# A graph layer on one core: single-column copies of x by 16-bit addresses, VectorE's written as maxima, and more of them

## The chip, the core and the metric

The kernel runs on one core of a Trainium2 chip. The core's engines work side by side: TensorE (PE) multiplies matrices, VectorE (DVE) works on elements and reductions, ScalarE (ACT) on activation functions and copies, GpSimd (POOL) issues the gathers, and SyncE (SP) only issues DMAs. Each has its own queue of instructions and works it off in order. The metric is the device time in microseconds (us) of one execution; smaller is better.

## The reference

A layer of a graph network over 12,500 nodes with 64 features and 400,000 edges with 16 attributes each. The edges come sorted by their target `dst`; the sources `src` are in random order.

```python
m_in = concatenate([x[src], x[dst], edge_attr], -1)       # 64 + 64 + 16
h = silu(m_in @ W1 + b1)                                  # 400000 x 64
messages = silu(h @ W2 + b2)
agg = segment_sum(messages, dst, num_segments=12500)
gnn = silu(concatenate([x, agg], -1) @ W3 + b3)
out = layernorm(x + gnn)
```

Everything is float32. The costly part is `x[src]`: 400,000 rows of 256 bytes at random places.

## The kernel before, in words

**Tiles.** The edges are cut into 3,125 tiles of 128. Eight tiles make an oct (1,024 edges), the unit of the main loop (391 octs, `for o in range(NO + 1)`). Three octs (24 tiles) make a window; since the edges are sorted by target, the targets of a window lie within 112 neighbouring nodes. Work on an oct is spread over several turns of the loop: its data are loaded two turns ahead (`load(o + 2)`), its messages are computed in turns o and o + 1, and summed in turn o + 2.

**Per oct.** SyncE loads `dr`, the target indices repeated over 112 partitions (L370, 448 KB), and the attributes into the lower part of `oh` (L372, 64 KB). VectorE makes the one-hot matrix `oh` of targets against the window's nodes (L381) and `eh`, its counterpart with edges on partitions (L388). TensorE multiplies `oh` with the window's `xw`, which holds x of the window's nodes by its part of W1 and the attributes' part below it (L401), and adds the sources' part (L412, L415). ScalarE makes `h` (L419), TensorE the second layer (L428, L430), ScalarE `m` (L434), and TensorE adds the messages by `eh` into a window's sums in PSUM (L443). At a window's end VectorE adds the sums into `agg` (L448), which holds all nodes. A window's own nodes are loaded by `window_load` (L347 register, L351 DMA), multiplied by `window_product` (L356) and put in place by `window_copy` (L360, L362). As soon as a group of nodes has all its sums, its last layer and layer norm are done between the octs (`node_load` to `store`, entered by `later`).

**Three ways to the sources' rows.** At the start TensorE multiplies all of x with the sources' part of W1 into a table `pa` in DRAM (`table`); the first 9 octs (`RAW`) gather from x itself.

1. *Gathers* (`gather`, L341): GpSimd fetches the 128 rows of a tile from `pa` with one indirect DMA into `ga`, three octs ahead, into five buffers. TensorE brings them into place by multiplying with the identity (L415).
2. *Columns* (`columns`, L267): x transposed stands in SBUF as `xs`, one column of 64 values for each node. An edge's column is copied from there by ScalarE or VectorE into `cx`, one instruction for each edge: 64 partitions by 4 bytes, with the source address in a register. 256 edges make a pair of tiles, which TensorE then multiplies with W1 (L412), and for which no gather is made. In each oct ScalarE copies 28 + 28 columns (`ACOLS`: one part before `h`, one before `m`), VectorE 24 + 24 (`VCOLS`). The addresses come as indices by a SyncE load (L319), are turned into addresses by VectorE (L327, two instructions for each pair, as the two halves of a pair read from two copies of x), and are loaded into the engines' registers by a TensorLoad (L263), at most 16 (`ALOAD`) at a time on ScalarE. 104 columns an oct make a pair for every 2.46 octs, 153 pairs in all.
3. *Rows* (`rows`, L292): SyncE fetches 16 rows of `pa` in each oct with 16 DMAs of one row, again by addresses in registers (L288). 23 pairs come this way.

**x in SBUF.** `xs` holds x transposed twice, on partitions 0 to 63 for even tiles and on 64 to 127 for odd ones. The address in a register has the partition in its upper bits (`XBASE`) and the byte in the partition, from 35,840 on (`XADDR`), in its lower ones; it is an int32. Seven loads for each copy (`resident`) are issued on SyncE's queue in the first octs.

**Order.** The order of instructions on PE, ACT, DVE and SP is that of the program text (`manual_schedule`); waits follow from the data and from the pools' buffers (`bufs`). GpSimd only gathers, and runs ahead as far as the five `ga` buffers let it. At the end the kernel makes sure that every edge was within its window; if not, a second general program does the work, which does not happen with this input.

## Time and profile before

| | us |
|---|---|
| median of 7 runs | 4874.31 (4853.41 to 4893.45) |
| profiled execution | 4867.82 |
| its span | 4866.0 |
| ScalarE busy | 2752.3 |
| VectorE busy | 2621.9 |
| GpSimd busy | 2648.1 |
| TensorE busy | 2936.0 |

The span is the time between the first and the last instruction in the profile. A row of the groups reads: line, engine, operation, what it writes and reads, how many, then busy time and the mean in ns of one, then the idle time of the engine just before these instructions and what ended most of it ("issue" is an idle time that ended by nothing that the profile shows; "remote" is a release by a semaphore whose sender isn't found). Register loads, semaphores and the issuing of DMAs aren't counted as busy. In the views of waits a row is the engine and line that waited, what for, then microseconds in all, times, and the longest. In the views of stretches each row is a stretch from and to, its length, then for PE, PEld (weight loads), DVE, ACT and POOL the busy time and the number of instructions, TensorE's granted clock, the share of the DMA engines and GB/s. In a timeline a row is the start, the length, engine, line, operation and count, and in brackets the idle time before.

### The profile page before, as it was taken

How to read it: one execution, taken by the hardware profiler on the slowest of the kernel's cores; microseconds unless marked ns; L12 is line 12 of the kernel's file. 1: busy time of each engine (PE TensorE's matmuls, PEld its weight loads, DVE VectorE, ACT ScalarE, POOL GpSimd, SP SyncE). 2: the span in 40 equal slices, each digit the busy share in tenths (PEclk: the TensorE clock that was granted, in tenths of full speed). 3: DMA queues.
4: the chain of work that ended last, by engine and by line, in shares of the span. 5: the costliest groups of instructions: out<-in, count | busy, mean ns of one | idle time of the engine just before them, and what ended most of it. 6: DMA issues, size and time to landing. Idle time of an engine off the chain costs nothing. (4 is left out here: it accounts for less than half of the span.)

```text
span 4866.0 us, 96997 instructions
## 1 busy us (share of the span) xinstructions
PE 2936.0 (60%) x15387; PEld 1956.7 (40%) x15387; DVE 2621.9 (54%) x19955; ACT 2752.3 (57%) x21941; POOL 2648.1 (54%) x2782
## 2 busy tenths in 40 slices
PE   4556656656666655665655556656655566566666
PEld 3334434434444443443433334434434344344444
DVE  1355555555555555555555555555555555555555
ACT  1255656656555555555555565555555556556554
POOL 5455555555555555555555555555555555555553
PEclk6766766666666666666666666676666666666667
DMA  4322222222222222222222222222222222222222
GB/s 104 95 65 66 62 65 66 67 65 66 65 69 69 66 65 65 66 62 67 68 60 70 64 67 66 66 66 66 62 64 71 66 66 65 64 62 66 68 72 55
DMA packets 199259, 327.19 MB, mean 67 GB/s; under 512 B 94959, under 2 KB 103306, under 8 KB 197722
## 3 DMA queue, kind: packets, MB, share of 16 engines
q1 hardware_dynamic: 96142, 226.51, 14.9%
q0 software_dynamic: 88736, 91.04, 10.7%
q10 hardware_dynamic: 13740, 3.32, 0.3%
q14 instruction: 511, 4.19, 0.3%
q8 instruction: 130, 2.13, 0.2%
HBM read 314.20 MB, written 6.40 MB: 66 GB/s over the span
## 5 line engine op out<-in xcount | busy, mean ns | idle before, releaser
L341 POOL DMA_INDIRECT ga<-pa,sc x2701 | 2578.8, 955 | 2112.5 <-PE p L415 1047.4
L267 ACT COPY cx<-xs 64x4 uint8 x21112 | 2270.1, 188 | 1421.3 <-issue 1363.7
L267 DVE COPY cx<-xs 64x4 uint8 x18056 | 1516.7, 192 | 781.6 <-issue 690.7
L443 PE MATMUL pg<-eh,m 128*64 128x112 f32 x6250 | 608.7, 365 | 1693.8 <-ACT m L434 812.2
L443 PEld LDWEIGHTS pg<-eh,m 128*64 128x64 f32 x6250 | 486.8, 201 | 1778.6 <-ACT m L434 851.4
L381 DVE TENSOR_TENSOR oh<-dr,wrow 112x1024 f32<-112x1024 int32 x391 | 476.0, 1217 | 907.9 <-DMA dr<-in_dst_row 567.5
L430 PE MATMUL p<-w2d,h 128*128 128x128 f32 x3126 | 719.2, 402 | 0.0
L430 PEld LDWEIGHTS p<-w2d,h 128*128 128x128 f32 x3126 | 617.0, 294 | 147.7 <-issue 147.7
L401 PE MATMUL p<-oh,xw 128*64 128x512 f32 x1564 | 645.7, 918 | 4.8 <-issue 4.8
L415 PEld LDWEIGHTS p<-ident,ga 128*128 128x128 f32 x2702 | 444.2, 247 | 304.6 <-issue 263.8
L415 PE MATMUL p<-ident,ga 128*128 128x128 f32 x2702 | 506.2, 341 | 0.0
L388 DVE TENSOR_TENSOR eh<-wrow,dc 128x896 f32<-128x896 f32 x391 | 424.4, 1085 | 140.6 <-issue 85.1
L419 ACT ACTIVATE h<-p,b1s 128x512 f32<-128x512 f32 x391 | 267.5, 684 | 297.7 <-remote 157.4
L434 ACT ACTIVATE m<-p 128x512 f32<-128x512 f32 x391 | 231.7, 593 | 344.0 <-remote 191.8
L428 PE MATMUL p<-b2r,one 3*128 3x512 bf16 x391 | 211.5, 541 | 0.0
L356 PE MATMUL mm<-w1ab,xr 64*112 64x64 f32 x262 | 76.3, 388 | 129.8 <-DMA xr<-in_xt 83.1
L412 PEld LDWEIGHTS p<-cx,w1d 128*128 128x128 f32 x306 | 59.8, 245 | 199.8 <-issue 199.8
L401 PEld LDWEIGHTS p<-oh,xw 128*64 128x64 f32 x1564 | 103.1, 182 | 67.2 <-issue 38.9
L356 PEld LDWEIGHTS mm<-w1ab,xr 64*112 64x112 f32 x262 | 53.2, 257 | 161.1 <-DMA xr<-in_xt 108.5
L341 POOL DMA_INDIRECT ga<-in_x,sc x72 | 68.1, 946 | 51.6 <-PE mm L406 29.3
L412 PE MATMUL p<-cx,w1d 128*128 128x128 f32 x306 | 95.4, 403 | 0.0
L448 DVE TENSOR_TENSOR agg<-agg,pg 128x112 f32 x131 | 34.8, 266 | 94.2 <-issue 39.0
(73 smaller groups left out, 734.2 us busy)
## 6 DMA issues: line engine op xcount, KB each, us to landing
dr<-in_dst_row SPq DMA_DIRECT2D x390, 448.0 KB
rx<-pa SPq DMA_DIRECT2D x5888, 0.2 KB
ga<-pa,sc POOLq DMA_INDIRECT x2701
oh<-in_attr_t SPq DMA_DIRECT2D x390, 64.0 KB
xs<-in_xt SPq DMA_DIRECT2D x12, 512.0 KB
xr<-in_xt SPq DMA_DIRECT2D x131, 28.0 KB
pa<-v ACTq DMA_DIRECT2D x24, 128.0 KB
xa<-in_x SPq DMA_DIRECT2D x24, 128.0 KB
```

The lines of the kernel that those rows point to most:

```text
L267: copy(t[h, 4 * e:4 * e + 4], xb[h, ds(r - (XBASE[s] + XADDR), 4)])
L341: nc.gpsimd.indirect_dma_start(out=ga[:, i, :], out_offset=None, in_=x if o < RAW else pa[:, :], in_offset=bass.IndirectOffsetOnAxis(ap=sc ...
L381: nc.vector.tensor_tensor(oh[0:W, :n2 * P], dr[:, :n2 * P], wn[0:W, c:c + 1].to_broadcast([W, n2 * P]), op=OP.is_equal)
L388: nc.vector.tensor_tensor(eh[:, :n], winrow[c][:, None, :].to_broadcast([P, n, W]), dc[:, t0:t0 + n, None].to_broadcast([P, n, W]), op=OP. ...
L401: nc.tensor.matmul(p1[s * D:(s + 1) * D, :k], xw[c % 3], ohv[:, s, :k], start=True, stop=False, skip_group_check=True)
L412: nc.tensor.matmul(p1[:, 0, :], w1d, cols.pop(o), start=False, stop=False, skip_group_check=True)
L415: nc.tensor.matmul(p1[:, i, :], g2.rearrange("p s d -> p (s d)"), ident, start=False, stop=(i == k - 1), skip_group_check=True)
L419: nc.scalar.activation(h[:, :k], p1[:, :k], AF.Silu, bias=b1s)
L428: nc.tensor.matmul(p2[:, :n2, :], one3, b2r[:, :n2, :], start=True, stop=False, skip_group_check=True)
L430: nc.tensor.matmul(p2[:, 2 * i:2 * i + 2, :].rearrange("p s d -> p (s d)"), h[:, i, :], w2d, start=False, stop=(i == k - 1), skip_group_ch ...
L434: nc.scalar.activation(m[:, :n2], p2[:, :n2], AF.Silu)
L443: nc.tensor.matmul(pg[s * D:(s + 1) * D, :], m[:, i, :], eh[:, i, :], start=(first and i < 2), stop=(last and i >= n - 2), skip_group_chec ...
```

## The change

All of it concerns the second way, the columns, and what stands around it:

- x transposed stands once in SBUF, on partitions 0 to 63, and at the front of it (pool `front`, from byte 8,864 of a partition on). Both halves of a pair read from it. The addresses fit in 16 bits; VectorE writes them with one instruction for each pair into a 16-bit tile `cxa` (L333), and the register loads read 16-bit words.
- VectorE's column copies become `tensor_reduce` with a maximum over one byte (L273); ScalarE's stay copies (L275).
- ScalarE copies 32 + 32 columns in an oct, VectorE 32 + 24. 120 columns make a pair for every 2.13 octs, 177 pairs instead of 153. So there are 24,192 copies instead of 21,112 on ScalarE, 21,120 instead of 18,056 on VectorE, and 48 gathers less.
- The loads of x into SBUF, now seven instead of 14, and the second load of `dc` go from SyncE's to ScalarE's queue.
- `ehp` has five buffers instead of four, `win` three instead of two, `cxi` two instead of three. A window's load stands one oct earlier; its product stands at the head of the turn before its first oct, ahead of the columns, instead of at the end of the turn before that; the window's sums are added one oct later, and the node work follows by one oct more.
- The scratch tiles of the check at the end lie in `agg` instead of `xs`. The ring in SBUF for the descriptors of GpSimd's DMAs is 8,192 bytes instead of 16,384, which lets x begin so far in front.

```diff
-ACOLS = (28, 28)
-VCOLS = (24, 24)
+ACOLS = (32, 32)
+VCOLS = (32, 24)
-XBASE = (0, 64 << 18)
-XADDR = 35840
+XADDR = 8864
...
+    front = ctx.enter_context(tc.tile_pool(name="front", bufs=1))
+    xs = front.tile([D, NP], F32, name="xs")
...
-    def resident(s, c):
+    def resident(c):
         w = min(XC, NP - c)
-        nc.sync.dma_start(xs[s * D:(s + 1) * D, c:c + w], xt[:, c:c + w])
+        nc.scalar.dma_start(xs[:, c:c + w], xt[:, c:c + w])
...
-            tc.tile_pool(name="ehp", bufs=4) as ehp, \
-            tc.tile_pool(name="work", bufs=2) as work, tc.tile_pool(name="win", bufs=2) as win, \
+            tc.tile_pool(name="ehp", bufs=5) as ehp, \
+            tc.tile_pool(name="work", bufs=2) as work, tc.tile_pool(name="win", bufs=3) as win, \
...
                 _, regs = nc.values_load_multi_w_load_instructions(
-                    indices[j][0:1, e0:e0 + n], engines=(eng,), min_val=XBASE[s] + XADDR,
+                    addresses[j][0:1, e0:e0 + n], engines=(eng,), min_val=XADDR,
...
                 for e, r in zip(range(e0 % P, e0 % P + n), regs):
-                    copy(t[h, 4 * e:4 * e + 4], xb[h, ds(r - (XBASE[s] + XADDR), 4)])
+                    to, frm = t[h, 4 * e:4 * e + 4], xb[:, ds(r - XADDR, 4)]
+                    if eng == ENG.DVE:
+                        nc.vector.tensor_reduce(to, frm[:, :, None], AX.X, OP.max)
+                    else:
+                        nc.scalar.copy(to, frm)
...
-                t = indices[j]
-                for s in range(2):
-                    h = slice(s * P, (s + 1) * P)
-                    nc.vector.tensor_scalar(t[:, h], t[:, h], 4.0, float(XBASE[s] + XADDR), op0=OP.mult, op1=OP.add)
+                addresses[j] = cxa.tile([1, 2 * P], U16, name="cxa")
+                nc.vector.tensor_scalar(addresses[j], indices.pop(j), 4.0, float(XADDR), op0=OP.mult, op1=OP.add)
...
                 if o == 8:
-                    nc.sync.dma_start(dc[:, SCT:], dst_c[:, SCT:])
+                    nc.scalar.dma_start(dc[:, SCT:], dst_c[:, SCT:])
...
-                    if octs[o + 2][3]:
-                        window_load(octs[o + 2][0])
+                if o + 3 < NO and octs[o + 3][3]:
+                    window_load(octs[o + 3][0])
+                if o and o + 1 < NO and octs[o + 1][3]:
+                    window_product(octs[o + 1][0])
                 if o + 1 < NO:
                     compare_dst(o + 1)
                 columns(o, ENG.DVE, 0)
-                if o >= 3 and octs[o - 3][4]:
-                    add_window(octs[o - 3][0])
+                if o >= 4 and octs[o - 4][4]:
+                    add_window(octs[o - 4][0])
...
-                if o + 2 < NO and octs[o + 2][3]:
-                    window_product(octs[o + 2][0])
...
-    nc = bacc.Bacc("TRN2", target_bir_lowering=False, num_devices=1)
+    nc = bacc.Bacc("TRN2", target_bir_lowering=False, num_devices=1, dynamic_dma_scratch_size=8192)
```

More of the change, by code (lines that the diff above doesn't have):

```diff
@@ L13 @@
 U8 = mybir.dt.uint8
+U16 = mybir.dt.uint16
 AF = mybir.ActivationFunctionType
@@ L102, in windows @@
     assert W + A == P and N + W <= NP
+    front = ctx.enter_context(tc.tile_pool(name="front", bufs=1))
+    xs = front.tile([D, NP], F32, name="xs")
+    assert XADDR + 4 * N < 1 << 16
     const = ctx.enter_context(tc.tile_pool(name="fconst", bufs=1))
@@ L164, in windows @@
     XC = 2048
-    xs = fast.tile([P, NP], F32, name="xs")
-    def resident(s, c):
+    def resident(c):
         w = min(XC, NP - c)
-        nc.sync.dma_start(xs[s * D:(s + 1) * D, c:c + w], xt[:, c:c + w])
+        nc.scalar.dma_start(xs[:, c:c + w], xt[:, c:c + w])
     def table(c):
@@ L176, in table @@
             o = c + i * P
-            nc.tensor.matmul(ps[:, i, :], xs[0:D, o:o + P], w1ab[:, 0, :], start=True, stop=True)
+            nc.tensor.matmul(ps[:, i, :], xs[:, o:o + P], w1ab[:, 0, :], start=True, stop=True)
         t = v[:, c // (4 * P) % (2 * RB)]
@@ L227, in windows @@
             tc.tile_pool(name="psa", bufs=1, space=PSUM) as psa, \
-            tc.tile_pool(name="cx", bufs=4) as cx, tc.tile_pool(name="cxi", bufs=3) as cxi, \
+            tc.tile_pool(name="cx", bufs=4) as cx, tc.tile_pool(name="cxi", bufs=2) as cxi, tc.tile_pool(name="cxa", bufs=4) as cxa, \
             tc.tile_pool(name="rx", bufs=2) as rx, tc.tile_pool(name="rxi", bufs=2) as rxi, \
@@ L240, in windows @@
             pairs.append(o)
-        cols, indices = {}, {}
+        cols, indices, addresses = {}, {}, {}
         xb = xs.bitcast(U8)
@@ L248, in columns @@
             if eng == ENG.Activation:
-                lo, n, copy = lo + sum(ACOLS[:part]), ACOLS[part], nc.scalar.copy
+                lo, n = lo + sum(ACOLS[:part]), ACOLS[part]
             else:
-                lo, n, copy = lo + sum(ACOLS) + sum(VCOLS[:part]), VCOLS[part], nc.vector.tensor_copy
+                lo, n = lo + sum(ACOLS) + sum(VCOLS[:part]), VCOLS[part]
             hi = lo + n
@@ L263, in columns @@
                 _, regs = nc.values_load_multi_w_load_instructions(
-                    indices[j][0:1, e0:e0 + n], engines=(eng,), min_val=XBASE[s] + XADDR,
-                    max_val=XBASE[s] + XADDR + 4 * (N - 1), skip_runtime_bounds_check_because="src names a node")
+                    addresses[j][0:1, e0:e0 + n], engines=(eng,), min_val=XADDR,
+                    max_val=XADDR + 4 * (N - 1), skip_runtime_bounds_check_because="src names a node")
                 for e, r in zip(range(e0 % P, e0 % P + n), regs):
-                    copy(t[h, 4 * e:4 * e + 4], xb[h, ds(r - (XBASE[s] + XADDR), 4)])
+                    to, frm = t[h, 4 * e:4 * e + 4], xb[:, ds(r - XADDR, 4)]
[3 more added lines that the diff above has]
+                        nc.scalar.copy(to, frm)
                 lo += n
@@ L472, in node_product @@
             av = agg[:, c:c + n].rearrange("k (p i) -> k i p", i=G)
-            xv = xs[0:D, c:c + n].rearrange("k (p i) -> k i p", i=G)
+            xv = xs[:, c:c + n].rearrange("k (p i) -> k i p", i=G)
             nc.tensor.matmul(po[:p], ones[:, :p], b3r, start=True, stop=False, skip_group_check=True)
@@ L527, in windows @@
         for q in range(early):
-            o = lead[due[q]] + 2
+            o = lead[due[q]] + 3
             later(o, node_load, q)
@@ L531, in windows @@
             later(o, node_silu, q)
-            later(o + 1, node_stats, q)
+            later(o + 2, node_stats, q)
         for q0 in range(0, rest, RB):
-            o = lead[due[q0 + RB - 1]] + 2
-            later(o + 2, root, q0, q0 + RB)
-            later(o + 3, inverse, q0, q0 + RB)
+            o = lead[due[q0 + RB - 1]] + 3
+            later(o + 3, root, q0, q0 + RB)
+            later(o + 4, inverse, q0, q0 + RB)
             for r in range(RB):
-                later(o + 3 + 2 * r, divide, q0 + r)
-                later(o + 4 + 2 * r, store, q0 + r)
+                later(o + 4 + 2 * r, divide, q0 + r)
+                later(o + 5 + 2 * r, store, q0 + r)
         for o in range(min(AHEAD, NO)):
@@ L563, in windows @@
                     for c in parts[:3] if o == 0 else parts[o + 2:o + 3]:
-                        resident(0, c)
+                        resident(c)
                 if o == 8:
-                    nc.sync.dma_start(dc[:, SCT:], dst_c[:, SCT:])
+                    nc.scalar.dma_start(dc[:, SCT:], dst_c[:, SCT:])
                 if o == RAW:
@@ L569, in windows @@
                     nc.vector.memset(eps, 1e-5)
-                if 5 <= o < 5 + (len(parts) + 1) // 2:
-                    for c in parts[(o - 5) * 2:(o - 4) * 2]:
-                        resident(1, c)
                 index(o + 3)
@@ L609, in windows @@
                         f(*a)
-        off = xs[:, :TILES]
+        off = agg[:, :TILES]
         full = (TILES // CT) * CT
@@ L620, in windows @@
         nc.gpsimd.iota(evi, pattern=[[STEP, NCH]], base=0, channel_multiplier=0)
-        lag = xs[:, TILES:TILES + NCH]
+        lag = agg[:, TILES:TILES + NCH]
         nc.vector.tensor_tensor(lag, evi, wb, op=OP.subtract)
@@ L637, in windows @@
         add_up(NO - 1)
-        for o in range(NO - 2, NO):
+        for o in range(NO - 3, NO):
             if octs[o][4]:
```

## The prediction

> **What bounds the kernel now.** I read the page's totals first, then the costliest groups, then what each engine waits for between 300 and 4,700 us (start and end left out), then single stretches in the order of time. The totals and the groups:

> ```profile
> PE 2936.0 (60%) x15387; PEld 1956.7 (40%) x15387; DVE 2621.9 (54%) x19955; ACT 2752.3 (57%) x21941; POOL 2648.1 (54%) x2782
> L341 POOL DMA_INDIRECT ga<-pa,sc x2701 | 2578.8, 955 | 2112.5 <-PE p L415 1047.4
> L267 ACT COPY cx<-xs 64x4 uint8 x21112 | 2270.1, 188 | 1421.3 <-issue 1363.7
> L267 DVE COPY cx<-xs 64x4 uint8 x18056 | 1516.7, 192 | 781.6 <-issue 690.7
> L381 DVE TENSOR_TENSOR oh<-dr,wrow 112x1024 f32<-112x1024 int32 x391 | 476.0, 1217 | 907.9 <-DMA dr<-in_dst_row 567.5
> ```

> No engine is busy over 60%, so the bound is in how the instructions follow each other. 4,866 us over 391 octs is 12.44 us for an oct. The waits, engine by engine:

> ```profile
> ACT cx L267 <- issue: 1295.1, 1894, 5.5
> ACT m L434 <- remote: 169.4, 46, 7.7
> ACT h L419 <- remote: 119.0, 34, 5.5
> ```

> ```profile
> POOL ga L341 <- PE p L415: 1012.4, 223, 14.5
> POOL ga L341 <- issue: 641.0, 2098, 0.6
> ```

> ```profile
> SPq L292 <- DMA rx<-pa: 54.8, 113, 1.4
> SPq L319 <- ACTq L263: 3.1, 11, 0.7
> ```

> GpSimd waits 1,012 us for a gather buffer that TensorE has still to read: its train of about 7 gathers an oct (a pitch of 1.25 us, 8.7 us in all) is not the end. ScalarE waits for almost nobody; what it loses, 1,295 us, stands before column copies and is called "issue": the data are there, the instruction isn't given out. SyncE's queue also waits for next to nothing. So the two queues that work by register, ScalarE's (56 copies an oct) and SyncE's (16 row copies an oct), run without a pause and set the pace together. I followed the chain of releases back from the end to 300 us: of 4,560 us about half lie on ScalarE (issue before copies 1,178, register loads 600, copies 519) and about 1,850 on SyncE's row copies and loads.

> What "issue" is shows in the order of time. ScalarE in two neighbouring stretches of equal work, the first at the head of a train of gathers, the second deep in it:

> ```profile
> 2404.10:2407.80 3.70, 2.31 (x25) 1.83 (x25) 0.69 (x7) 3.65 (x34) 3.04 (x3) 1.00 0.50 159
> 2409.30:2415.40 6.10, 0.69 (x7) 0.49 (x5) 2.06 (x24) 1.74 (x10) 3.97 (x4) 0.83 0.16 28
> ```

> ```profile
> 2411.93 0.19 ACT L267 COPY cx<-xs 64x4 uint8 x1 [0.43 <-issue]
> 2412.64 0.19 ACT L267 COPY cx<-xs 64x4 uint8 x1 [0.51 <-issue]
> 2413.36 0.19 ACT L267 COPY cx<-xs 64x4 uint8 x1 [0.53 <-issue]
> 2414.06 0.19 ACT L267 COPY cx<-xs 64x4 uint8 x1 [0.51 <-issue]
> ```

> The third busy column is VectorE, the fourth ScalarE, the fifth GpSimd. 34 instructions in 3.70 us against 10 in 6.10: one or two copies each 0.71 us. Over the whole run ScalarE starts 9 to 10 instructions a microsecond in the first two gathers of a train, 2.7 in the fourth, 2.0 to 1.3 from the fifth on, and 9 again after the train. One gather late in a train so costs ScalarE about 1.25 x (1 - 2/9) = 0.97 us.

> **The change part by part** (sum against the profiled execution, 4,867.8 us; the median of the runs is 4,874.3, 6.5 more).

> *8 more columns on each of two engines.* In fast stretches ScalarE's copies follow at 95 ns. 24,192 - 21,112 = 3,080 copies x 0.095 = 293 us if every one lies on the path, nothing if SyncE's chain covers them all. Half of the chain is ScalarE's, so I take half: +146. On VectorE 3,064 more at 71 ns are 218 us; they lie beside 638.6 us of its own issue idle and 565.3 us of waiting for `dr`, so 0 as long as VectorE keeps that slack (1,204 us over the run).

> *Fewer gathers.* 177 pairs instead of 153: 24 x 2 = 48 gathers less, each 0.97 us of slow ScalarE: -47 (0 if the slow part starts by the clock and not by the count).

> *16-bit addresses.* A register load of 16 words takes 1,017 ns on ScalarE, one of 12 takes 783: 58.8 ns a register and 75 fixed. They are these:

> ```profile
> L263 ACTq TENSOR_LOAD <-cxi x1602: 305/787/1210, 206.1 to 4813.8; - x178
> L263 DVEq TENSOR_LOAD <-cxi x847: 591/1600/1806, 198.5 to 4794.8; - x170
> ```

> No row shows a 16-bit load, so two bounds. Unchanged by the register: the 600 us on the chain grow by 64/56, +86. Halved by the byte: 16 registers cost 0.545 us, and 600 x 64/56 x 0.54 = 370, -230. But only 172 us of the loads' 1,365 us fall where ScalarE's unit is idle, and a gain on ScalarE beyond a point only leaves SyncE's row copies as the end, with half of the chain. I take the halved price, as the time per register is already proportional to the words fetched, and half of its gain: -115.

> *One-byte maxima for VectorE's copies.* Their price: a VectorE instruction on one element follows the next at 60 ns, a 131-element reduction at 196, so 64 ns is my estimate for 4 elements against 71 for the copy. VectorE's sum per oct is then 56 x 64 = 3.6 against 48 x 71 = 3.4 us: nothing. For others: a gather with five or more of VectorE's copies beside it took 0.973 us, one with none 0.945 (pitches 1.272 and 1.250). In ticks of late gathers ScalarE starts 2.17 copies per gather without VectorE copies beside them and 1.7 with. Taking the pitch alone, 0.022 x 2,653 = 58 us less gathering, at most 45 for ScalarE; I take -30 (bounds 0 and -80, the latter with half a copy more per slow gather, 0.47 x 4 x 0.11 us x 382).

> [...]

> *Bulk loads on ScalarE's queue, one copy of x.* Seven of SyncE's 512-KB loads vanish, seven and one load of `dc` move past SyncE's `dr` and `oh` loads to ScalarE's queue, all before oct 9 when ScalarE has no copies and is 20% busy. Gathers pause there for 22, 9 and 31 us; I take a quarter of these 62, -15 (bounds 0 and -60). Behind the moved issues on ScalarE stand the first SiLUs, for 8 issues.

> *Index loads and addresses.* 24 more 1-KB loads on SyncE's queue (a row copy takes it 0.32 us in fast stretches, so about 8 us, half on the chain: +4). On VectorE 177 address operations replace 306 of 243 ns: -30, under VectorE's slack, 0.

> *Window loads an oct earlier, products, sums and node work an oct later, a fifth `eh`, a third `xr` buffer.* The waits that they concern (PE's products for `xr` 83 us, VectorE's `xw` copy 54.6 us remote) are off ScalarE and SyncE: 0 taken, -40 at best. If a cover goes, the product now stands at the head of the oct on TensorE, where the first layer is queued behind it: 131 x 0.39 us x 2 = 100 us at worst, less TensorE's 1,690 us of idle before the sums.

> *The descriptor ring, 8,192 instead of 16,384 bytes.* Gathers land 2.1 us after their start at a pitch of 1.25, two in flight; no row shows a full ring. 0; if half the ring started the slow part one gather earlier, 0.97 us x 382 = +370. That is the upper bound of an unknown, far from the rows.

> Sum: +146 - 47 - 115 - 30 - 15 + 4 = -57: 4,867.8 - 57 + 6.5 = 4,817. As several bounds reach further down than up around ScalarE's loads, I say **4,805 us**.

> **The rivals.**
> - *A. The loads of registers are hidden and ScalarE simply copies more* (slower). Place: ScalarE's fast stretches. All 3,080 copies count, +293, 16-bit loads give nothing, -47 for gathers: 4,874 + 246 = 5,120; with half of the ring's or maxima's help, 5,000 to 5,120. For it: only 172 us of loads in idle time, and copies back to back at 95 ns. Against: 600 us of loads on the chain. It decides once the loads and maxima give ScalarE less than 0.76 us an oct (8 x 95 ns).
> - *B. The slow ticks go with VectorE's copies or with the word loads* and the trains no longer starve the queues. Even a third of the 1,295 us of issue would give -430 + 146: about 4,590. For it: 2.17 against 1.7 copies per late gather. Against: ticks where VectorE is still.
> - *C. SyncE's row copies alone set the end* (no change): 16 rows an oct before and after, ScalarE's extra work under them; 4,860 to 4,890. Against: TensorE waits 759 us for ScalarE's `m` on the sums, so ScalarE is often last.
> - *D. The maxima are dear.* VectorE's slack, 1,204 us over 21,120 operations, is used up when one costs 57 ns more than a copy; at twice that it would be the bound, about +1,200. [...]

> **How the numbers follow.** My forecast (some per cent faster, 4,720 to 4,850) 0.41; B 0.14; A 0.33; C 0.07; D and the ring 0.05. About 0.3%, 15 us, is what a measurement of this kernel can tell from no change. Faster: 0.41 + 0.14, and a part of C, 0.56; same 0.05; slower 0.39. Range: 4,590 (B) to 5,090, which leaves out the ring, D and the upper end of A. The forecast's own range is 4,720 to 4,850.

> **What would show each step.** Loads: L263's median on ScalarE near 430 ns, not 787. Copies: ScalarE's issue idle well under 1,295 us with 24,192 copies. Maxima: about 64 ns apart, gathers at 1.25 us with them beside. Ticks of 0.71 us in late gathers should remain, some 2% fewer. `dr` waits unchanged. I am wrong if loads keep 58.8 ns a register and the period grows by 0.6 us or more (A), or if ticks start a gather sooner (ring), or if ScalarE's "issue" falls by a third (B).

## The result and the profile after

The changed kernel takes 6,599.8 us (median of 19 runs, 6,580.8 to 6,633.6) against 4,871.4 us (46 runs): a ratio of 1.355, 95% interval 1.353 to 1.357. It is 35% slower where some per cent faster were forecast; the time is outside the range.

The totals and the groups of the changed kernel, in the columns described above:

```profile
PE 2950.4 (45%) x15387; PEld 1973.4 (30%) x15387; DVE 2557.3 (39%) x22890; ACT 2979.6 (45%) x25019; POOL 2573.4 (39%) x2734
L347 POOL DMA_INDIRECT ga<-pa,sc x2653 | 2504.0, 944 | 3886.3 <-PE p L421 2879.7
L275 ACT COPY cx<-xs 64x4 uint8 x24192 | 2485.6, 188 | 3222.3 <-issue 3172.6
L273 DVE TENSOR_REDUCE cx<-xs 64x4 uint8 x21120 | 1462.4, 140 | 3654.7 <-issue 3605.5
```

No engine works longer than the counts explain: ScalarE copies 24,192 columns at the same 188 ns, VectorE's maxima take 140 where its copies took 192. What grew is the idle time in front of both, called "issue": from 1,364 to 3,173 us on ScalarE, from 691 to 3,606 on VectorE. Neither engine waits much for another; by far the longest wait of each is this one (from 300 to 6,400 us):

```profile
ACT cx L275 <- issue: 3055.4, 1672, 4.7
DVE cx L273 <- issue: 3479.0, 1212, 6.4
```

The others wait for these two: SyncE for VectorE's `oh`, GpSimd for TensorE, TensorE for ScalarE's `m` and VectorE's `agg`:

```profile
SPq L376 <- DVE oh L387: 1650.2, 269, 10.4
POOL ga L347 <- PE p L421: 2781.0, 265, 21.3
PE pg L449 <- DVE agg L454: 1593.9, 119, 18.9
PE pg L449 <- ACT m L440: 844.6, 109, 14.9
```

SyncE, whose largest wait before was 54.8 us in all (from 300 to 4,700 us), now waits 1,650 us for `oh`. What stands in that idle time is seen in the register loads, which aren't counted as busy (duration minimum, median, maximum in ns):

```profile
L266 ACTq TENSOR_LOAD <-cxa x1608: 1706/3372/3645, 203.4 to 6533.1; - x179
L266 DVEq TENSOR_LOAD <-cxa x870: 1821/5349/7362, 195.8 to 6518.9; - x174
```

Before, the medians were 787 and 1,600 ns at nearly the same number of loads; a load of 16 registers on ScalarE took 1,017 ns and now takes 3,372. The sum over all of ScalarE's loads went from 1,365 to 5,118 us. In the order of time ScalarE now has a rhythm (changed kernel, start, length, and in brackets the idle time before):

```profile
3000.70 1.62 ACT L275 COPY cx<-xs 64x4 uint8 x16
3004.65 1.62 ACT L275 COPY cx<-xs 64x4 uint8 x16 [2.33 <-issue]
3006.18 0.58 ACT L440 ACTIVATE m<-p 128x512 f32<-128x512 f32 x1
3008.72 1.62 ACT L275 COPY cx<-xs 64x4 uint8 x16 [1.95 <-issue]
3012.69 1.62 ACT L275 COPY cx<-xs 64x4 uint8 x16 [2.35 <-issue]
```

Sixteen copies each 4.0 us. The records of the trace give the load for the second group: it starts at 3,001.21, 0.50 us after the first copy of the group before it, when ten copies are still to be started, and lasts 3.37 us. Those ten, 95 ns apart, cover about 1.0 us of the load and no more. A load of 1.02 us, as 32-bit words take, hides under them; one of 3.37 leaves about 2.3 us open. Over the run from 300 to 6,400 us, 3,010 of the loads' 4,927 us fall where ScalarE's unit is idle; before, from 300 to 4,700 us, it was 172 of 1,300. 24,192 copies are 1,512 groups of 16; the loads run from 203 to 6,533 us, which is 4.19 us a group. So ScalarE's rhythm fills the whole span but for the start. VectorE's loads, 4,711 us in all, run beside it.

### The profile page after: what moved, and what is told of

The parts are those of the page before. It is cut to its first block, busy times and chain, and to the rows that moved or that the text cites. A ratio compares the mean times of both kernels' runs of the same rounds, so it can differ in the third digit from the quotient of the medians.

```text
span 6588.9 us, 102561 instructions
## 1 busy us (share of the span) xinstructions
PE 2950.4 (45%) x15387; PEld 1973.4 (30%) x15387; DVE 2557.3 (39%) x22890; ACT 2979.6 (45%) x25019; POOL 2573.4 (39%) x2734
## 3 DMA queue, kind: packets, MB, share of 16 engines
q1 hardware_dynamic: 94926, 218.59, 10.6%
q8 instruction: 130, 2.13, 0.1%
## 5 line engine op out<-in xcount | busy, mean ns | idle before, releaser
L347 POOL DMA_INDIRECT ga<-pa,sc x2653 | 2504.0, 944 | 3886.3 <-PE p L421 2879.7
L275 ACT COPY cx<-xs 64x4 uint8 x24192 | 2485.6, 188 | 3222.3 <-issue 3172.6
L273 DVE TENSOR_REDUCE cx<-xs 64x4 uint8 x21120 | 1462.4, 140 | 3654.7 <-issue 3605.5
L387 DVE TENSOR_TENSOR oh<-dr,wrow 112x1024 f32<-112x1024 int32 x391 | 473.2, 1210 | 85.6 <-issue 78.9
L425 ACT ACTIVATE h<-p,b1s 128x512 f32<-128x512 f32 x391 | 266.8, 682 | 162.3 <-issue 54.6
L434 PE MATMUL p<-b2r,one 3*128 3x512 bf16 x391 | 214.9, 550 | 0.0
L418 PE MATMUL p<-cx,w1d 128*128 128x128 f32 x354 | 113.8, 414 | 0.0
L483 PE MATMUL mm<-w3s,agg 128*128 128x64 f32 (+1 forms) x200 | 71.5, 457 | 0.0
L482 PE MATMUL mm<-w3x,xs 64*128 64x64 f32 (+1 forms) x200 | 71.1, 454 | 0.0
L434 PEld LDWEIGHTS <-one 3*128 3x128 bf16 x391 | 37.8, 97 | 96.0 <-issue 82.5
```

The costliest lines, as they stand in the source:

```text
L273: nc.vector.tensor_reduce(to, frm[:, :, None], AX.X, OP.max)
L275: nc.scalar.copy(to, frm)
L347: nc.gpsimd.indirect_dma_start(out=ga[:, i, :], out_offset=None, in_=x if o < RAW else pa[:, :], in_offset=bass.IndirectOffsetOnAxis(ap=sc ...
L387: nc.vector.tensor_tensor(oh[0:W, :n2 * P], dr[:, :n2 * P], wn[0:W, c:c + 1].to_broadcast([W, n2 * P]), op=OP.is_equal)
L425: nc.scalar.activation(h[:, :k], p1[:, :k], AF.Silu, bias=b1s)
L434: nc.tensor.matmul(p2[:, :n2, :], one3, b2r[:, :n2, :], start=True, stop=False, skip_group_check=True)
```

## The experiments

The runs were made in five sets, each with its own runs of the kernel before, and this kernel came out in two ways: 4,872, 4,992 and 4,877 us in the sets e, h and i, as in the profile above, and 3,555 and 3,557 us in the sets f and g. The ticks of the prediction are stretches in which ScalarE starts one or two copies each 0.71 us; in the second kind they are all but missing. A column copy of ScalarE started 0.60 to 0.76 us after the one before 1,298 times in the profile before and 1,418 times in h2, but 90 times in f4, which is h2's kernel. Ratios are therefore always against the kernel before in the same set, and "with ticks" or "without ticks" is named. The record numbers the chip of each set: 13, 10 and 12 with ticks (e, h, i), 12 and 14 without (f, g). Number 12 stands on both sides, so either two chips bear it or the difference does not belong to a chip; which of the two isn't known. TensorE's granted clock differs too (0.67 in h2, 0.75 in f4), but where ScalarE copies without ticks it is as fast in both kinds: 28 copies took 2.71 to 2.84 us in the profile before, at a granted clock of 0.67, and 32 took 3.22 us in f4, 97 to 101 ns each. So a slower ScalarE isn't the reason.

**e1: 32-bit words for the register loads.**

```diff
-                addresses[j] = cxa.tile([1, 2 * P], U16, name="cxa")
+                addresses[j] = cxa.tile([1, 2 * P], I32, name="cxa")
```

> The changed kernel with one edit: the address tile cxa is int32, so that the register loads read 32-bit words again; front of SBUF, one copy of x, 120 columns, maxima, queues and order stay. Theory (the price of a 16-bit register load, 3,372 ns for a load on ScalarE instead of 787, is the whole loss): the loads fall back to about 1,000 ns for 16 registers, ScalarE's issue idle to 1,300 us or less, and the time to 4,750 to 5,100 us. Rival 1 (the loss is in 120 columns or in the new order of the window's work): above 6,000 us with cheap loads. Rival 2 (the smaller descriptor ring or x at the front makes register loads and copies slow): loads stay above 3,000 ns, 6,600 us.

Measured, with ticks: 5,120.9 us, ratio 1.052 (1.047 to 1.058). One type in one line is 1,479 of the 1,728 us lost; the time is 21 us above the upper end expected. The loads of this version, and ScalarE's wait from 300 to 4,900 us:

```profile
L266 ACTq TENSOR_LOAD <-cxa x1608: 542/1020/1312, 205.0 to 5065.1; - x179
L266 DVEq TENSOR_LOAD <-cxa x870: 591/1603/2392, 197.7 to 5048.3; - x174
```

```profile
ACT cx L275 <- issue: 1225.0, 1844, 5.1
```

The loads are those of before again, with x in front and with the small ring. Rivals 1 and 2 are out. 249 us above the kernel before stay, and the sets from f on ask for them.

**e2: 16-bit loads from words 4 bytes apart.** The addresses are written as int32, and the loads read the lower half of each.

```diff
-                addresses[j] = cxa.tile([1, 2 * P], U16, name="cxa")
-                nc.vector.tensor_scalar(addresses[j], indices.pop(j), 4.0, float(XADDR), op0=OP.mult, op1=OP.add)
+                words = cxa.tile([1, 2 * P], I32, name="cxa")
+                addresses[j] = words.bitcast(U16).rearrange("o (e h) -> o e h", h=2)
+                nc.vector.tensor_scalar(words, indices.pop(j), 4.0, float(XADDR), op0=OP.mult, op1=OP.add)
...
-                    addresses[j][0:1, e0:e0 + n], engines=(eng,), min_val=XADDR,
+                    addresses[j][0:1, e0:e0 + n, 0], engines=(eng,), min_val=XADDR,
```

> The changed kernel with addresses written as int32 and loaded as 16-bit words, every second one: the width of the load stays 16 bits, but each address has 4 bytes of its own. If the price goes by the width of the word (about 206 ns a register), 16 registers still take 3,372 ns and the time stays at 6,600 us. If two addresses in one 4-byte word are what costs, the loads fall to about 1,000 ns and the time to that of the 32-bit version.

Measured in a single run: 6,604.7 us, and

```profile
L266 ACTq TENSOR_LOAD <-cxa x1608: 1704/3372/3673, 203.0 to 6547.1; - x179
```

the same 3,372 ns. It is the 16-bit width of the load, not two addresses in one word.

**e3: 16-bit loads with the column counts of before** (`ACOLS = (28, 28)`, `VCOLS = (24, 24)`).

> The changed kernel with 28 + 28 and 24 + 24 columns, as before the change; 16-bit loads stay. Theory (dear loads): 56 registers for ScalarE in an oct instead of 64, at 206 ns 1.65 us an oct less, and 8 copies of 95 ns less, so 6,600 - 382 x 2.4 = about 5,700 (all on ScalarE's path) to 5,950 us. Rival 1 (120 columns are what is too many): 4,900 us.

Measured in a single run: 5,849.7 us, within the expected 5,700 to 5,950. The fewer columns don't bring the time of before. Loads of 4, 8, 12 and 16 registers take 0.88 (e3's shortest), 1.71, 2.57 (e3's median) and 3.37 us in e3 and the changed kernel: from 4 to 16, 207 ns a register and some 50 fixed, against 59 and 75 for 32-bit words.

**e4: the kernel before with maxima on VectorE.**

```diff
-                    copy(t[h, 4 * e:4 * e + 4], xb[h, ds(r - (XBASE[s] + XADDR), 4)])
+                    to, frm = t[h, 4 * e:4 * e + 4], xb[h, ds(r - (XBASE[s] + XADDR), 4)]
+                    if eng == ENG.DVE:
+                        nc.vector.tensor_reduce(to, frm[:, :, None], AX.X, OP.max)
+                    else:
+                        copy(to, frm)
```

> The kernel before with one edit: VectorE's column copies as one-byte maxima. Theory: the maxima follow at 65 ns instead of 71 and take no part in the loss; gathers fall from 955 to 945 ns; 4,871 us within 1%, rather below. Rival 3 (maxima are dear, VectorE's 3,600 us of idle before them in the changed kernel is theirs): 5,500 us or more.

Measured, with ticks: 4,927.6 us, ratio 1.011 (1.005 to 1.017). Rival 3 is out; but the maxima, forecast at -30 us, cost some 54. The gathers did what was expected: 955 ns fell to 946. The time is lost elsewhere: from 300 to 4,700 us VectorE waits 770 us for `dr` instead of 565, and ScalarE 244 us before `m` for a release whose sender isn't found, instead of 169.

**f1 to f4: the 249 us taken apart.** f1 is e1 with 28 + 28 and 24 + 24 columns, f2 is e1 with `nc.vector.tensor_copy(to, frm)` in place of the maximum, f3 is both, and f4 is the kernel before with 32 + 32 and 32 + 24 columns.

> The changed kernel with 32-bit register loads and 28 + 28 and 24 + 24 columns. It asks where the 249 us go that the 32-bit version is still above the kernel before (5,121 against 4,872). Theory (16 more columns an oct, 8 of them on ScalarE at 95 ns): 4,870 to 4,930 us, with VectorE's maxima left. Rival (the order of the window's work, the queues, the smaller ring): still 5,050 us or more.

> The changed kernel with 32-bit register loads and VectorE's columns as copies again; 120 columns an oct stay. From the kernel before with maxima alone (4,928, 56 us above its neighbour): 5,121 - 56 = about 5,065 us if the maxima cost the same here. [...]

> The changed kernel with 32-bit register loads, 104 columns as 28 + 28 and 24 + 24, and VectorE's columns as copies: what is left of the change is one copy of x at the front, the ring of 8,192 bytes, the bulk loads on ScalarE's queue, the buffers and the order of the window's work. Theory (these are worth little): 4,850 to 4,890 us. Rival (they cost, by the window's product at the head of a turn): above 4,950 us; or they gain: below 4,830.

> The kernel before with 32 + 32 and 32 + 24 columns and nothing else. Theory (each column more on ScalarE lies on its path): 4,872 + 382 x 8 x 0.095 - 47 for 48 gathers = about 5,115 us. If SyncE's row copies cover half of it: about 4,990. If copies instead of gathers are worth it: under 4,860.

This set fell where the kernel before takes 3,555.1 us, and the order is reversed: f1 3,526.7 (0.991, 0.989 to 0.993), f2 3,461.7 (0.974, 0.972 to 0.976), f3 3,525.0 (0.992, 0.990 to 0.994), f4 3,489.6 (0.982, 0.980 to 0.984). No expectation was made for this. ScalarE's wait in f4 from 300 to 3,300 us, and two engines in the same microseconds, show why:

```profile
ACT cx L267 <- issue: 97.3, 243, 0.7
```

```profile
2002.68 0.95 POOL L341 DMA_INDIRECT ga<-pa,sc  x1 [0.30 <-issue]
2003.93 0.94 POOL L341 DMA_INDIRECT ga<-pa,sc  x1 [0.30 <-issue]
2005.18 0.94 POOL L341 DMA_INDIRECT ga<-pa,sc  x1 [0.30 <-issue]
2006.43 0.94 POOL L341 DMA_INDIRECT ga<-pa,sc  x1 [0.30 <-issue]
```

```profile
2002.04 3.22 ACT L267 COPY cx<-xs 64x4 uint8 x32 [0.41 <-issue]
2005.17 0.58 ACT L434 ACTIVATE m<-p 128x512 f32<-128x512 f32 x1
2005.66 3.21 ACT L267 COPY cx<-xs 64x4 uint8 x32
```

ScalarE copies 32 columns without a gap (in 3.22 us; its issue idle is 97 us and not 1,295), although gathers run under it all the time, and GpSimd hardly pauses (in g4, the same kernel, never over 0.3 us from 300 to 3,300 us): its train of 1.25 us a gather is the end here. 48 gathers less are 48 x 1.25 = 60 us; f4 gained 66 and f1 to f2, 16 columns more with copies for maxima, 65. Maxima and copies are alike (f1 and f3, 0.991 and 0.992).

**g1 to g4: the changed kernel, e1, f3 and f4 in one set.**

> The changed kernel as it is, once more, together with three others on one chip, as the second group of runs was on a chip where the kernel before takes 3,555 us and not 4,872, its sequencers give out instructions without the ticks of 0.71 us, and GpSimd has no pause between its gathers. Theory (the 16-bit loads cost 206 ns a register on every chip, and ScalarE's queue has 64 an oct, 13.2 us, which nothing can hide): where the kernel before takes 3,555 us, ScalarE's sequence of loads and copies still sets the end, 6,300 to 6,600 us; where it takes 4,870, 6,600. Rival (the loads are slow only where the ticks are): 3,400 to 3,500 us on a chip without ticks.

> The changed kernel with 32-bit register loads, once more. On a chip with ticks 5,121 us, ratio to the kernel before 1.05, as before; on a chip without, where the gathers are the end and 48 of them are gone: about 3,462 us as with VectorE's copies, plus or minus 20, ratio 0.97 to 0.98.

> What is left of the change without 16-bit loads, maxima and 16 more columns, on one chip with the others. On a chip without ticks its ratio was 0.992. On a chip with ticks, theory (order, queues, ring and one copy of x are worth nothing there): 0.99 to 1.01. Rival (they carry part of the 5 per cent that the 32-bit version loses there): 1.02 or more.

> The kernel before with 120 columns an oct. On a chip without ticks its ratio was 0.982, since gathers are the end there. On a chip with ticks, theory (ScalarE's issue is the end, and 8 copies of 95 ns an oct lie on it): 1.03 to 1.055. Rival (more columns pay there too): 0.98 to 1.00.

Again without ticks, before 3,557.4 us: the changed kernel 6,277.2 (1.765, 1.762 to 1.768), e1's kernel 3,466.0 (0.974, 0.973 to 0.976), f3's 3,522.3 (0.990), f4's 3,488.4 (0.981). The changed kernel is 23 us under the 6,300 expected, e1's within its range. The changed kernel's loads have a median of 3,371 ns there too, and from 300 to 6,000 us

```profile
ACT cx L275 <- issue: 2890.6, 1449, 3.1
PE pg L449 <- ACT m L440: 2883.9, 351, 11.3
```

TensorE waits for ScalarE almost alone (17 us for VectorE). 1,512 groups of 16 copies at 4.0 us are 6,050 us of 6,277. So the price of the 16-bit loads does not hang on the ticks, and without that price the change is 2.6% faster than before where there are no ticks. With VectorE's copies in place of the maxima (f2) the ratio is the same, 0.974.

**h1 to h4.** h1 is f3's kernel, h2 is f4's, h4 the kernel before with 24 + 24 and 20 + 20 columns. h3 shortens the trains of gathers to four:

```diff
-                if o in (pairs, rpairs)[i // 2 % 2] and i < 4:
+                if i < 4 and (o >= RAW and n == OT or o in (pairs, rpairs)[i // 2 % 2]):
                     continue
...
-                g2 = single.pop(o) if o in rpairs and i == 1 else ga[:, 2 * i:2 * i + 2, :]
+                q = 2 + i % 2 if n == OT else i
+                g2 = single.pop(o) if o in rpairs and i == 1 else ga[:, 2 * q:2 * q + 2, :]
```

> What is left of the change without 16-bit loads, maxima and 16 more columns. On two chips without ticks its ratio was 0.990 and 0.992. On a chip with ticks, theory (order, queues, ring and one copy of x are worth nothing there): 0.99 to 1.01. Rival (they carry part of the 5 per cent that the 32-bit version loses there): 1.02 or more.

> The kernel before with 120 columns an oct. On two chips without ticks its ratio was 0.981, since gathers are the end there. On a chip with ticks, theory (ScalarE's issue is the end, and 8 copies of 95 ns an oct lie on it): 1.03 to 1.055. Rival (more columns pay there too): 0.98 to 1.00.

> The kernel before with only the last four tiles of each full oct gathered from oct 9 on; the first layer reads their rows in place of those left out, so that the sources of the other tiles are wrong and every other instruction stays. It asks whether the ticks belong to long trains of gathers: they begin at about the fourth gather of a train. Theory: with trains of four, ScalarE's issue idle falls from 1,295 us to under 400, and the time on a chip with ticks to 3,500 to 3,900 us, though GpSimd wasn't the end. Rival (the ticks are a matter of the chip and come whatever is gathered): 4,700 us or more. On a chip without ticks: 3,150 to 3,350, ScalarE's sum of 8 us an oct.

> The kernel before with 24 + 24 and 20 + 20 columns: 88 an oct, about 50 gathers more. On a chip with ticks, theory (ScalarE's issue is the end): 8 copies of 95 ns less, 12 per cent of its fast work, and longer trains: 0.95 to 0.985. On a chip without ticks, where the gathers set the end: 1.015 to 1.025.

With ticks, before 4,991.6 us: h1 1.020 (1.014 to 1.027), h2 1.028 (1.024 to 1.032), h4 1.022 (1.019 to 1.026), h3 4,011.9 us in a single run. ScalarE's wait in h3 from 300 to 3,900 us, and some of its gathers:

```profile
ACT cx L267 <- issue: 428.7, 745, 2.7
```

```profile
2018.40 0.94 POOL L341 DMA_INDIRECT ga<-pa,sc  x1 [3.00 <-PE p L416]
2019.65 0.94 POOL L341 DMA_INDIRECT ga<-pa,sc  x1 [0.31 <-issue]
2020.90 0.94 POOL L341 DMA_INDIRECT ga<-pa,sc  x1 [0.30 <-issue]
2022.15 0.94 POOL L341 DMA_INDIRECT ga<-pa,sc  x1 [0.30 <-issue]
```

Leaving out 1,172 of the 2,701 gathers, and nothing else, takes two thirds of the issue idle and 980 us away, from a kernel whose GpSimd was waiting for others. The ticks come with the gathers; the time is 110 us above what was expected.

By the place of a gather in its train, ScalarE starts 8.8, 9.4, 7.2 and 2.6 instructions a microsecond (register loads included) under the first four of the kernel before and 1.9 to 1.1 under the fifth to the eighth. In h3 the four places give 6.3, 10.3, 7.4 and 2.0: the fourth is as slow as before, and what is gone are the places behind it. A long train alone isn't enough: f4's gathers follow each other without a break, and ScalarE starts 8.0 a microsecond under them. And the two kinds part before any column is copied: h2's second `h` starts at 65.8 us and f4's, of the same kernel, at 33.2, the first column copies at 194 and 123 us.

h2 shows that 16 more columns cost 2.8% with ticks (the lower edge of the expected 3.0 to 5.5) where they gain 1.9% without. h4 was expected faster and is slower: with 88 columns ScalarE's issue idle in the page falls from 1,364 to 1,012 us, but VectorE waits 1,260 us for `dr`, SyncE's load, instead of 568. 104 is better than both neighbours with ticks. h1's two per cent are outside the 0.99 to 1.01 of its theory and at the edge of its rival (1.02 or more).

**i1: h1 with a ring of 14,336 bytes** (`XADDR = 15008`, `dynamic_dma_scratch_size=14336`), and **i2: a pause after each gather** (`nc.gpsimd.memset(pause, 0.0)`, 128 x 128, in the kernel before).

> What is left of the change without 16-bit loads, maxima and 16 more columns, but with a descriptor ring of 14,336 bytes instead of 8,192 (x then begins at byte 15,008). With the small ring it was at a ratio of 1.020 on a chip with ticks and 0.990 to 0.992 on two without. Theory (the small ring costs there): below 1.010 on a chip with ticks. Rival (the order of the window's work or ScalarE's queue does): 1.015 to 1.025. On a chip without ticks 0.99 either way.

> The kernel before with a memset of 128 x 128 on GpSimd after each gather from oct 9 on, which spaces the gathers of a train by about 0.2 to 0.3 us more (a pitch of 1.5 us instead of 1.25; 7.06 of them are 10.6 us of the 12.4 us of an oct). Theory (ticks come when gathers follow each other without a pause for more than three): ticks begin later or not at all, ScalarE's issue idle falls below 800 us, and on a chip with ticks the time falls to 4,200 to 4,700 us. Rival (the number of gathers in flight doesn't matter, only their number): the slow stretch is longer, 5,000 us or more. On a chip without ticks GpSimd is the end and it is slower: 10.6 us an oct, about 4,150 us, ratio 1.15 to 1.2.

With ticks, before 4,876.9 us: i1 1.019 (1.016 to 1.022). With most of the ring given back the 1.9% stay as the rival had it, so the ring is not what costs h1 its 2.0%. i2 came to 5,452.7 us (1.119), but it did not do what it was made for: the order of GpSimd's instructions isn't written out by hand, and up to 102 memsets stand in one block, mostly after each six or eight gathers, until they are used up at about 1,180 us; after that the gathers follow each other as before. It tells nothing on spacing, and whether the ticks would start later in a train with wider gaps stays open.

## Why the prediction was wrong

**16-bit addresses: -115 forecast, +1,479 measured (e1). This is the step that failed.** It was bounded by "unchanged by the register" (+86) and "halved by the byte" (-230), and the halved price was taken "as the time per register is already proportional to the words fetched". The rows had shown durations for loads of several counts, but for one width only; they said nothing on another width, and the upper bound was a guess of no change, not a bound. None of the signs of being wrong named a load that costs more. In its place: 207 ns a register instead of 59, by width alone (e2: a median of 3,372 ns with the words 4 bytes apart), with ticks (3,372) and without (g1: 3,371). Why a 16-bit word costs more was not shown.

**"Only 172 us of the loads' 1,365 us fall where ScalarE's unit is idle"** was a right reading (172 of 1,300 us from 300 to 4,700 us; 1,365 is the whole run), and hid how near its end the cover was. Here a load lies hidden under the copies that are still to be started when it begins: in the changed kernel mostly ten (813 of its 1,546 loads on ScalarE from 300 to 6,400 us, as the copies that follow without a pause), 1.0 us, which is what a 32-bit load of 16 takes (1.02 us). So the cover was about full, as an estimate from these two numbers. A longer load lies open beyond it: of 3.37 us, 2.3 us, and 3,010 us from 300 to 6,400 us. The number that mattered was how much longer a load could become before it showed, not how much of it showed now.

**8 more columns on each engine, and 48 gathers fewer: +146 - 47 = +99 forecast.** h2 has both alone: +2.8% of 4,991.6, +139 us. The sign held, the size was some 40 us low. The mechanism isn't shown by it: the same prices for h4, 2,952 copies fewer and 46 gathers more on the same path, give about -140 + 45 = -95 us, and h4 measured +113. Without ticks the edit is worth -66 us (f4).

**Maxima: -30 forecast, +54 with ticks (e4), nothing without (f1 against f3).** The price of one was right (64 ns from one to the next, the median in the changed kernel). The gain for the gathers came, and was worth nothing: with copies, a gather with five or more of them beside it took 973 ns before, with maxima 946 (e4), and yet e4 is slower. In the new layout nothing is left to gain: gathers take 944 to 947 ns with maxima (e1, f1) and with copies (f2, f3, h1). In e4 VectorE's waits for `dr` grew by 205 us and ScalarE's before `m` by 74; why maxima lengthen them was not settled.

**Bulk loads, order, buffers, ring: -15 forecast (0 each for order and ring).** h1 shows +2.0% with ticks, f3 and g3 -0.8 and -1.0% without. The ring is out as far as i1's 14,336 of 16,384 bytes tell; between the order of the window's work, the buffers, the queues and the single copy of x it stays open.

**The rivals.** A gave 5,120 us, and e1's 5,121 looks like it, but is not only A: A put it all on ScalarE's copies, while columns (139), maxima (54) and the rest (101) are 294 us one by one, in two sets, against 249 together. A's condition, loads at their old price, did not hold for the changed kernel. B supposed that the ticks would go with cheaper loads. They did become rarer (120 starts of a copy 0.60 to 0.76 us after the one before, against 1,298), where some 2% fewer were forecast, but the loads' pauses of 2.3 us stood in their place; that was no gain. That VectorE's copies make the ticks is out too: in the profile before VectorE starts nothing from 2,411.7 to 2,415.5 us while ScalarE's copies keep their 0.71 us, and in e4, with maxima, ScalarE's issue idle before copies is 1,272 us against 1,295. C is out by h2. D is out by e4.

**The reading of what bounds the kernel** fits the sets with ticks: ScalarE's issue in ticks beside SyncE. h4 and its `dr` waits fit SyncE's share of it, since less work for ScalarE brought nothing. That the same kernel also runs without ticks, with GpSimd's gathers as the end, could not be seen from one trace.

## What to carry to other kernels

A row gives a price for the form it shows; an operand type that no row shows is unbounded until it is measured, even where the new type is smaller, and a change that rests on it should be tried with that one type alone first. Of a cost that is hidden, ask how much it may grow before its cover ends: here the cover was ten copies still to be started, one microsecond, beside a load of 1.02 us. Under a train of gathers ScalarE's instructions can come slowly in one set of runs and not in another (8.8 a microsecond under a train's first gather and 1.9 to 1.1 under its fifth to eighth in the kernel before, 8.0 in f4), so numbers of copies against gathers should be tuned over several sets, each with the kernel before beside it.
